# A banded product in four 64x64 tiles of TensorE, in two stacked banded layers (one core of a Trainium2)

## The chip, the cores and the metric

The kernel runs on one NeuronCore of one Trainium2 chip. The metric is the device time of one execution in microseconds; the time before the change is 4874.15 us, the median of 3 runs (4872.71 to 4876.42). In the profile PE is TensorE's matmuls, PEld its weight loads, DVE VectorE, ACT ScalarE, POOL GpSimd and SP the SyncE queue, which here issues nearly all DMAs.

## The reference

The input x is 512 x 512 positions of 64 channels. Two layers of one form follow each other, each with weights of its own:

```python
def layer(x):                                  # x: (1, 512, 512, 64)
    xn   = ln(group_norm(x, 32 groups))        # per position, over 64 channels
    left  = (xn @ Wl + bl) * mask * sigmoid(xn @ Wlg + blg)     # 64 -> 128
    right = (xn @ Wr + br) * mask * sigmoid(xn @ Wrg + brg)
    gate  = sigmoid(xn @ Wog + bog)
    out = 0
    for dd in range(-4, 5):                    # band of nine rows
        out[i, j] += left[i + dd, i] * right[i + dd, j]          # per channel
    out = ln(out) * gate
    return x + out @ Wo + bo                   # 128 -> 64
```

The statistics of the group norm run over the whole image, so the second layer can begin its work only when the first is through. The band couples only the nine rows around row i, and of left only the positions (i + dd, i) near the diagonal are needed. For one channel, the sum over dd is a product of a banded 64 x 64 matrix (from left) with rows of right.

## The kernel before, in words

**Tiling.** The 512 rows are cut into nine blocks of 64 rows that overlap by eight. A tile holds on its 128 partitions the 64 rows of a block twice: partitions 0 to 63 for a column j, 64 to 127 for column j + 256. These are the two halves, `e` = 0 and 1 in the code. A *unit* is 8 columns of each half, a *chunk* 16 units (128 columns of each half), so a layer has 18 chunks or 288 units. All arithmetic is fp32.

**One step.** `layer` (line 718) writes out one unit step after the other; nearly every instruction is recorded through one helper at line 373, which keeps all of them in program order, so the profile shows L373 everywhere and groups are told apart by tiles. In step t of a layer:

- `affine`, `inner_stats`, `inner_norm` (427 to 440): group norm and layer norm of z on POOL, statistics on DVE. `solve` (577), every fourth step, turns the statistics into the scales: five small instructions on DVE (var, nm, rs), then a chain of ten to twelve on POOL (rsqrt, rs, nm).
- `transposed`, `kept` (442, 461): PE transposes z into PSUM, ACT copies it to SBUF as zT (adding 1.0, by which the biases enter the products), SP stores zT to `later` in DRAM.
- `right` (488), `right_gate`, `right_end`: twice per step, PE multiplies zT by the right weights and their gate weights (4 matmuls of 64 rows x 128 columns of weights, 256 moving columns), ACT takes the sigmoid (sg), DVE multiplies into RO.
- `mix` (544): the band product, for 8 channels of a chunk. Per channel and half one matmul of 64 x 64 weights (A, from left) and 128 moving columns of RO; result in two PSUM banks, then copied back over RO, one half by ACT and one by DVE. 16 mixes per chunk, laid out over ten of its 16 steps as 2,1,2,2,1,2,1,2,2,1 (line 743).
- `out_stats`, `norm` (571, 610): statistics of the product on DVE, normalisation on ACT (eight instructions of 128 x 128 per step, tile `on`).
- `recall`, `gates`, `gated` (619 to 645): zT read back 30 steps later as zg, multiplied by the gate weights, sigmoid on ACT.
- `turned`, `times_gate`, `end` (647 to 695): transposes of the normalised product, times gate on DVE (ZH), times Wo on PE. `fetch`, `biased`, `ended`: x is fetched into XR, biased on POOL, added on DVE, stored by SP. In layer 0 `sums` (706) adds up on PE the statistics for the next group norm.

**Left.** `left` (502) runs in steps 3, 5, 7, 9 and 11 of each layer for the 36 near-diagonal positions, and writes its result to DRAM (`left_of`), in the layout in which `take_left` (532) fetches 16 channels (a *slab*) into a tile A of 64 positions x 16 channels per partition, the same for both halves.

**What sets the order.** Each engine works its own list in program order. The lists follow the order of the calls in the loop of `layer`. `count` (line 761) says how many units' affines fall in each of a chunk's 16 steps: 1,1,2,1,2,1,1,2,1,1,1,0,1,1,0,0. PSUM has eight banks: two pairs (`two_banks`, line 131) that right, transposed and mix share, and single ones (`one_bank`, line 128) for gates, turned and end: three in layer 0 (an eighth bank holds the sums), four in layer 1. A request waits until the oldest tile of its ring is free.

Of the kernel before, what the change touches and what calls it, by code (L numbers as in the profile page):

```python
# [8 lines left out]
F32 = mybir.dt.float32  # L9
# [10 lines left out]
S = 64  # L20
# [59 lines left out]
def tile_two_banded_layers(  # L80
# [28 lines left out]
    slab = S * (S + 2 * WIN) * HA  # L109
    size = H // HA * slab  # L110
# [350 lines left out]
    def kept(u: Unit):  # L461
        u.t = ztp.tile([P, JU // 2, P], F32, tag="zT", name="zT")
        to = u.t.rearrange("c k (n p) -> c n k p", n=2)
        for n, pt in enumerate(u.pt):
            en.scalar.activation(
                to[:, n : n + pt.shape[1]], pt.rearrange("c n (k p) -> c n k p", p=S),
                AF.Identity, bias=1.0,
            )
        if u.near is None:
            en.sync.dma_start(later[u.at], u.t)  # L470
# [5 lines left out]
    def projected(u: Unit, q: int, w: bass.AP):  # L476

        pr = two_banks().rearrange("p (e k h) -> p e k h", e=2, k=JQ // 2)
        for k in range(JQ // 2):
            for e in range(2):  # L480
                part = slice(e * D, (e + 1) * D)
                en.tensor.matmul(
                    pr[:, e, k, :], lhsT=u.t[part, q // 2 + k, :], rhs=w[part],
                    start=True, stop=True,
                )
        return pr

    def right(u: Unit, q: int, w: dict):
        u.pr[q] = projected(u, q, w["right"]).rearrange("p e k h -> p (e k) h")
# [12 lines left out]
    def left(u: Unit, q: int, w: dict):  # L502

        n0 = u.near + q
        pr = projected(u, q, w["left"])
        sg = wk.tile([P, JQ, H], F32, tag="sg", name="sg", bufs=2)
        sl = sg.rearrange("p j h -> p (j h)").rearrange("p (s j x) -> p s j x", j=JQ, x=HA)
        sv = sl.rearrange("p s (k e) x -> p e k s x", e=2)
        for e in range(2):
            en.scalar.activation(  # L510
                sv[:, e], pr[:, e, :, H:].rearrange("p k (s x) -> p k s x", x=HA), AF.Sigmoid
            )
        near = w["near"][:, n0 : n0 + JQ].unsqueeze(1).unsqueeze(3)
        en.gpsimd.tensor_tensor(sl, sl, near.broadcast_to([P, H // HA, JQ, HA]), ALU.mult)
        for e in range(2):
            en.vector.tensor_tensor(
                sv[:, e], pr[:, e, :, :H].rearrange("p k (s x) -> p k s x", x=HA), sv[:, e],
                ALU.mult,
            )
        for o, r, k, m in runs(n0, n0 + JQ):  # L520
            for n, b in enumerate(blocks):
                q0 = b.s // JQ
                at = n * size + (r * (S + 2 * WIN + 1) + k) * HA
                en.sync.dma_start(
                    strided(
                        left_of, at, (JQ * (S + 2 * WIN + 1) * HA, S // JQ), (slab, H // HA),
                        (1, m * HA),
                    ),
                    sl[q0 : q0 + S // JQ, :, o : o + m, :].rearrange("q s j x -> q s (j x)"),
                )  # L530

    def take_left(n: int, h: int) -> bass.AP:


        A = lp.tile([P, S, HA], F32, tag="A", name="A")
        at = n * size + h * slab + WIN * HA
        for e in range(2):
            en.sync.dma_start(
                A[e * S : (e + 1) * S].rearrange("p i h -> p (i h)"),
                strided(left_of, at, ((S + 2 * WIN) * HA, S), (1, S * HA)),  # L540
            )
        return A

    def mix(c: int, A: bass.AP, h0: int) -> list:


        j0 = c % 2 * (JC - JW)
        R = RO[:, :, j0 : j0 + JC, :]
        pb = two_banks()
        ph = pb.rearrange("i (h j) -> i h j", j=JC)  # L550
        for turn in range(2):
            for h in range(HB // 2):
                for e in range(2):
                    part = slice(e * S, (e + 1) * S)
                    hh = (turn ^ e) * (HB // 2) + h
                    en.tensor.matmul(
                        ph[part, hh, :], lhsT=A[part, :, h0 % HA + hh],
                        rhs=R[part, (h0 + hh) // 2, :, hh % 2],
                        start=True, stop=True,
                    )  # L560
        q = HB // 4
        v = [pb.rearrange("i (h t j) -> i h j t", t=2, j=JC)[:, n * q : (n + 1) * q] for n in range(2)]
        return [(R[:, h0 // 2 + n * q : h0 // 2 + (n + 1) * q], v[n]) for n in range(2)]
# [154 lines left out]
    def layer(src: bass.AP, dst: bass.AP, w: dict, stats: bool, then=None):  # L718
# [60 lines left out]
        for t in range(min(loads), last_t + 3):  # L779
# [37 lines left out]
            if t in units:  # L817
                right(units[t], 0, w)
            if t in outs:
                gates(outs[t], w)  # L820
            for v in looking[0:2]:
                out_stats(*v)
            if t in units:
                right_gate(units[t], 0)
            for u in inputs(t + 2):
                inner_norm(u)
            if t in units:
                right_end(units[t], 0)
            if t in outs:
                gated(outs[t])  # L830
# [4 lines left out]
            if t in units:  # L835
                right(units[t], JQ, w)
            for v in looking[2:5]:
                out_stats(*v)
            if t in outs:
                turned(outs[t], w)  # L840
            for u in inputs(t + 1):
                transposed(u)
            for u in then_affine:
                affine(u, en.gpsimd)
            then_affine = []
            if stats and t - 2 in outs:
                sums(outs[t - 2], t - 2 == first_t, t - 2 == last_t)
            for v in looking[5:]:
                out_stats(*v)
            if t - 1 in outs:  # L850
                end(outs[t - 1], w)
            if t in units:
                right_gate(units[t], JQ)
            if t + 1 in outs:
                norm(outs[t + 1], 0, 4)
            for u in inputs(t + 1):
                kept(u)
            if t in units:
                right_end(units[t], JQ)
            for v in todo:  # L860
                inner_stats(*v)
            if len(mixing) > 0:
                c, h0 = mixing[0]
                mixed.append(mix(c, A[c, h0 // HA], h0))
# [6 lines left out]
            if t in outs:  # L871
                times_gate(outs[t], w)
            if len(mixing) > 1:
                c, h0 = mixing[1]
                mixed.append(mix(c, A[c, h0 // HA], h0))
            if t + 1 in outs:
                norm(outs[t + 1], 4, 8)
            if len(mixing) > 0:
                en.scalar.copy(*mixed[0][0])
            if len(mixing) > 1:  # L880
                en.scalar.copy(*mixed[1][0])
            if t - 1 in outs:
                ended(dst, outs[t - 1])
            if len(mixing) > 0:
                en.vector.tensor_copy(*mixed[0][1])
            if t in outs:
                biased(outs[t], w, stats)
# [78 lines left out]

    XR = [keep.tile([P, JU // 2, 2 * D + 2], F32, name=f"XR{i}") for i in range(4)]
# [56 lines left out]
```

## Time and profile before

| | us |
|---|---|
| median of 3 runs | 4874.15 |
| the profiled execution, its time | 4876.42 |
| its span in the profile | 4874.6 |
| statistics of the input (POOL idle, DVE at work) | 0 to 290 |
| start of layer 0, with `left` | 290 to 440 |
| first mixes | 440 to 550 |
| steady steps of layer 0 | 550 to 2400 |
| last steps of layer 0 | 2400 to 2600 |
| start of layer 1, first mixes | 2600 to 2870 |
| steady steps, then last steps of layer 1 | 2870 to 4710, to 4875 |

How to read it. The page gives for each engine its busy time and share of the span, then for the costliest groups the number of instructions, the busy time in us, the mean length of one in ns, and the engine's idle time just before them with its releaser. A table of stretches gives the busy time of every engine between two moments. An instruction's busy time can overlap its successor's on PE and ACT, so the sum over groups may exceed an engine's busy time. The view of waits names who waited for whom. In the timeline equal instructions that follow each other are merged (x32).

### The profile page before, as it was taken

To read this page: it belongs to the slowest core of one execution; us is meant where nothing else is said; L and a number is where in the kernel's file an instruction comes from. 1 tells how busy PE (TensorE), PEld (TensorE's weight loads), DVE (VectorE), ACT (ScalarE), POOL (GpSimd) and SP (SyncE) were. 2 spreads that over 40 slices of the span, in tenths; PEclk is the share of its full clock that TensorE was granted. 3 is DMA by queue.
4 is the path that set the end of the run, shared out by engine and by line. 5 is a ranking of instruction groups with operands and counts; after the bars stand their busy time and mean duration, and the time that the engine had idled before them with its cause. 6 is when DMAs were issued, how large, how long until landed. Compare 5 with 4: busy or idle time off the path is not lost.

```text
span 4874.6 us, 173394 instructions
## 1 busy us (share of the span) xinstructions
PE 4107.5 (84%) x67090; PEld 3507.8 (72%) x67090; DVE 3830.6 (79%) x9635; ACT 3642.8 (75%) x8156; POOL 3804.8 (78%) x4739
## 2 busy tenths in 40 slices
PE   1026899999999999999984589999999999999998
PEld 0014788888888888888863467777777777777786
DVE  6835788888888888888765578888888888888887
ACT  0013688888888888888872368888888888888888
POOL 0035899989999999999634589998999999998963
PEclk9987999999999999999996899999999999999999
DMA  7844577777777777777653457777777777777766
GB/s 302 338 161 118 164 212 212 211 207 211 207 215 211 209 208 210 212 212 213 188 161 86 118 166 215 209 211 205 209 208 213 211 208 209 207 211 212 218 191 172
DMA packets 905343, 982.31 MB, mean 202 GB/s; under 512 B 114210, under 2 KB 641608, under 8 KB 900168
## 3 DMA queue, kind: packets, MB, share of 16 engines
q1 hardware_dynamic: 899840, 969.73, 68.0%
q8 instruction: 530, 8.68, 0.8%
q14 instruction: 293, 2.40, 0.2%
q10 hardware_dynamic: 4680, 1.50, 0.1%
HBM read 658.42 MB, written 312.46 MB: 199 GB/s over the span
## 4 chain that ended last, share of the span: by engine, by line
PE 56%; DVE 15%; ACT 12%; POOL 6%; DMA 4%; issue 3%; SPq 3%; ACTq 0%; POOLq 0%; DVEq 0%
PE banks L373 36%; PE bank L373 18%; ACT on L373 6%; DVE gn_st L373 3%; POOL rsqrt L373 3%; DVE RO L373 3%; SPq L373 3%; PE acc L373 3%; DVE sto L373 3%; ACT gate L373 2%; ACT zT L373 2%; DVE sti L373 2%; DVE ZH L373 2%; ACT sg L373 1%; DVE var L373 1%
## 5 line engine op out<-in xcount | busy, mean ns | idle before, releaser
L373 ACT ACTIVATE on<-RO,nm,rs 128x128 f32<-128x128 f32 x4608 | 1924.3, 492 | 68.3 <-POOL nm L373 53.7
L373 PE MATMUL banks<-pack,zT 64*128 64x256 f32 x9360 | 1335.1, 407 | 358.1 <-ACT zT L373 281.3
L373 PEld LDWEIGHTS banks<-pack,zT 64*128 64x128 f32 x9360 | 893.5, 195 | 731.7 <-ACT zT L373 327.8
L373 PE MATMUL banks<-RO,A 64*64 64x128 f32 x18432 | 1154.5, 277 | 19.9 <-ACT zT L373 12.7
L373 PEld LDWEIGHTS banks<-RO,A 64*64 64x64 f32 x18432 | 1082.5, 183 | 46.9 <-ACT zT L373 15.2
L373 DVE TENSOR_TENSOR RO<-banks,sg 128x512 f32<-128x512 f32 x1152 | 788.2, 684 | 396.3 <-ACT sg L373 376.4
L373 ACT ACTIVATE sg<-banks 128x512 f32<-128x512 f32 (+1 forms) x1188 | 697.1, 588 | 421.9 <-PE banks L373 292.5
L373 DVE BATCH_NORM_STATS2 sto<-RO 128x6 f32<-128x256 f32 x2304 | 845.2, 413 | 1.2
L373 DVE SCALAR_TENSOR_TENSOR ZH<-bank,pack,gate 128x448 f32<-128x448 f32 (+1 forms) x1152 | 736.4, 681 | 44.6 <-ACT gate L373 27.8
L373 DVE COPY RO<-banks 128x512 f32<-128x512 f32 x576 | 397.8, 691 | 430.0 <-ACT RO L373 427.7
L373 POOL TENSOR_TENSOR z<-z,gb 128x512 f32<-128x512 f32 x536 | 686.0, 1280 | 42.0
L373 POOL TENSOR_TENSOR z<-z,ga 128x512 f32<-128x512 f32 x536 | 685.2, 1278 | 5.6 <-DMA z<-mid_x 2.4
L373 PE MATMUL bank<-pack,ZH 128*64 128x64 f32 x18432 | 651.4, 224 | 4.7 <-ACT gate L373 4.3
L373 POOL TENSOR_TENSOR z<-z,rs 128x512 f32<-128x512 f32 x586 | 613.1, 1046 | 46.0
L373 ACT ACTIVATE gate<-bank 128x448 f32<-128x448 f32 (+1 forms) x1152 | 570.3, 547 | 88.1 <-PE bank L373 81.9
L373 POOL TENSOR_TENSOR z<-z,sti 128x512 f32<-128x512 f32 x586 | 620.8, 1059 | 0.0
L373 PEld LDWEIGHTS bank<-pack,ZH 128*64 128x64 f32 x18432 | 587.2, 138 | 26.3 <-ACT gate L373 7.9
L373 PE MATMUL bank<-zg,pack 64*128 64x448 f32 (+1 forms) x2304 | 568.7, 561 | 2.6 <-DMA zg<-later 2.3
L373 ACT COPY RO<-banks 128x512 f32<-128x512 f32 x576 | 335.1, 582 | 284.3 <-PE banks L373 280.0
L373 DVE BATCH_NORM_STATS2 sti<-z 128x6 f32<-128x128 f32 x2344 | 504.2, 282 | 12.9 <-POOL z L373 12.7
L373 PEld LDWEIGHTS bank<-ident,on 64*128 64x128 f32 x9216 | 404.9, 139 | 125.7 <-ACT gate L373 36.7
L373 POOL TENSOR_TENSOR XR<-XR,pack 120x512 f32<-120x512 f32 (+1 forms) x352 | 417.8, 1189 | 86.5 <-DMA XR<-in_x_dram 32.0
(145 smaller groups left out, 3587.2 us busy)
## 6 DMA issues: line engine op xcount, KB each, us to landing
later<-zT SPq DMA_DIRECT2D x576, 256.0 KB
A<-left_of SPq DMA_DIRECT2D x576, 256.0 KB
zg<-later SPq DMA_DIRECT2D x576, 256.0 KB
z<-in_x_dram SPq DMA_DIRECT2D x576, 128.0 KB
z<-mid_x SPq DMA_DIRECT2D x576, 128.0 KB
gn_x<-in_x_dram SPq DMA_DIRECT2D x16, 4096.0 KB
XR<-in_x_dram SPq DMA_DIRECT2D x448, 112.0 KB
mid_x<-XR SPq DMA_DIRECT2D x448, 112.0 KB
```

The costliest lines, as they stand in the source:

```text
L373: return lambda *a, **k: tc.keep_in_program_order(f(*a, **k))
```

## The change

It does the same arithmetic with four edits.

1. **The band product in four tiles.** Of the 128 channels, half (`s` = 1) are kept with swapped halves: the row half e of RO holds for them the columns of half 1 - e. In `mix` the matmul for these channels reads rows of half e and writes partitions of half 1 - e (`to` = `e ^ s`), so that the four 64x64 tiles (row half, column half) are each addressed in turn, and the result comes out with its halves in place. `one_bank` is asked twice per mix, one bank for s = 0 and one for s = 1; `two_banks` is no longer used for it.
2. **`crossed`, in place of `projected`, for right.** The swapped channels are made at the projection: zT is kept with its first half once more behind the second (`P + S` columns, a third ACT copy in `kept`), and right's matmul for s = 1 takes the weights' window shifted by 64. There are eight matmuls of 128 moving columns per call instead of four of 256.
3. **Left as channel pairs.** `left` writes its product into L9, a view of the last 36 columns of RO, which are not in use yet, and sends it out when all nine positions of a row offset r are there. `take_left` fetches A as 8 pairs x 64 positions x 2, in four transfers per slab instead of two.
4. **Another order of the calls in a step.** `out_stats`, `inner_stats` and `solve` stand ahead of `gated` and `right_end`; `gates` and both `right` calls follow each other; the mixes come late, the second behind the second half of `norm`, with `sums` between `end` and the second mix.

From the programs' lists: SP issues 72 transfers `left_of<-RO` of 16 x 64 runs of 18 numbers in place of 216 `left_of<-sg` of 16 x 8 runs of 16 to 64 numbers, and 1152 `A<-left_of` of 64 x 4 runs of 128 numbers in place of 576 of 64 runs of 1024.

```diff
     def kept(u: Unit):
-        u.t = ztp.tile([P, JU // 2, P], F32, tag="zT", name="zT")
-        to = u.t.rearrange("c k (n p) -> c n k p", n=2)
+        u.t = ztp.tile([P, JU // 2, P + S], F32, tag="zT", name="zT")
+        to = u.t.rearrange("c k (n p) -> c n k p", n=3)
...
         if u.near is None:
-            en.sync.dma_start(later[u.at], u.t)
+            en.scalar.activation(
+                to[:, 2], u.pt[0][:, 0].rearrange("c (k p) -> c k p", p=S), AF.Identity, bias=1.0
+            )
+            en.sync.dma_start(later[u.at], u.t[:, :, :P])
...
+    def crossed(u: Unit, q: int, w: bass.AP):
+        pr = two_banks().rearrange("p (e k h) -> p e k h", e=2, k=JQ // 2)
+        for k in range(JQ // 2):
+            for s in range(2):
+                for e in range(2):
+                    part = slice(e * D, (e + 1) * D)
+                    en.tensor.matmul(
+                        pr[:, e, k, :].rearrange("p (g s x) -> p g s x", g=2, s=2)[:, :, s],
+                        lhsT=u.t[part, q // 2 + k, s * S : s * S + P],
+                        rhs=w[part].rearrange("c (g s x) -> c g s x", g=2, s=2)[:, :, s],
+                        start=True, stop=True,
+                    )
+        return pr
...
     def left(u: Unit, q: int, w: dict):
...
         for e in range(2):
             en.vector.tensor_tensor(
-                sv[:, e], pr[:, e, :, :H].rearrange("p k (s x) -> p k s x", x=HA), sv[:, e],
-                ALU.mult,
+                L9[:, :, n0 + e : n0 + JQ : 2, :],
+                pr[:, e, :, :H].rearrange("p k (h t) -> p h k t", t=2),
+                sv[:, e].rearrange("p k (h t) -> p h k t", t=2), ALU.mult,
             )
-        for o, r, k, m in runs(n0, n0 + JQ):
-            for n, b in enumerate(blocks):
...
+        for r in range(JQ):
+            if n0 < (r + 1) * NEAR <= n0 + JQ:
+                for n, b in enumerate(blocks):
...
     def take_left(n: int, h: int) -> bass.AP:
-        A = lp.tile([P, S, HA], F32, tag="A", name="A")
+        A = lp.tile([P, HA // 2, S, 2], F32, tag="A", name="A")
...
     def mix(c: int, A: bass.AP, h0: int) -> list:
...
-        pb = two_banks()
-        ph = pb.rearrange("i (h j) -> i h j", j=JC)
-        for turn in range(2):
-            for h in range(HB // 2):
-                for e in range(2):
-                    part = slice(e * S, (e + 1) * S)
-                    hh = (turn ^ e) * (HB // 2) + h
-                    en.tensor.matmul(
-                        ph[part, hh, :], lhsT=A[part, :, h0 % HA + hh],
-                        rhs=R[part, (h0 + hh) // 2, :, hh % 2],
-                        start=True, stop=True,
-                    )
+        ph = [one_bank().rearrange("i (h t j) -> i h t j", h=q, t=2) for s in range(2)]
+        for h in range(q):
+            for t in range(2):
+                for s in range(2):
+                    for e in range(2):
+                        part, to = (slice(n * S, (n + 1) * S) for n in (e, e ^ s))
+                        en.tensor.matmul(
+                            ph[s][to, h, t, :], lhsT=L[part, s, h, :, t], rhs=R[part, s, h, :, t],
+                            start=True, stop=True,
+                        )
...
+    L9 = RO[:, :, 2 * JC - JW - NEAR * JQ :, :]
```

The order of the calls in a step, steady part, each engine's own list (before, then after; "t" left out where it is the step's own unit):

```
PE    before: right0 gates right1 turned transposed(t+1) sums(t-2) end(t-1) mix mix
PE    after:  right0 gates right1 turned transposed(t+1) end(t-1) mix sums(t-2) mix
DVE   before: looks right_end0 looks right_end1 inner_stats solve times_gate ended copy copy
DVE   after:  looks inner_stats solve right_end0 times_gate right_end1 ended copy copy
ACT   before: sg0 gated sg1 norm kept norm copy copy
ACT   after:  sg0 gated sg1 norm kept kept' copy norm copy
POOL  before: inner_norm affine affine(t+1) rsqrt biased
POOL  after:  inner_norm affine rsqrt biased affine(t+1)
```

## The prediction

> **What bounds the kernel now.** I read the page's busy times first, then stretches from the middle of each layer, then one engine at a time: who waits, and for how long.
>
> ```profile
> PE 4107.5 (84%) x67090; PEld 3507.8 (72%) x67090; DVE 3830.6 (79%) x9635; ACT 3642.8 (75%) x8156; POOL 3804.8 (78%) x4739
> ```
>
> Five rows between 72% and 84% bound nothing by themselves. The table of stretches (PE, PEld, DVE, ACT, POOL busy us, then clock and DMA) does better:
>
> ```profile
> 1000.00:2000.00 1000.00, 963.97 (x17089) 853.27 (x17084) 834.46 (x2101) 866.50 (x1929) 912.95 (x1107) 1.00 0.74 210
> 3200.00:4200.00 1000.00, 918.65 (x14834) 785.64 (x14832) 843.03 (x2093) 856.01 (x1922) 911.96 (x1105) 0.98 0.74 209
> ```
>
> The first row is layer 0, the second layer 1, which does without the sums on PE: 45 us less PE busy, yet the same number of steps. The sg tile, two per step, counts 275 and 275 on ACT: 137.5 steps, 7.27 us each, 116.3 us for a chunk of 16. So PE, though busiest, does not set the pace alone. POOL's busy time leaves out a gap of some 80 ns behind most of its instructions; its waits are this (us, times, longest):
>
> ```profile
> POOL rsqrt L373 <- DVE rs L373: 32.8, 35, 1.9
> POOL z L373 <- DMA z<-in_x_dram: 0.9, 2, 0.5
> ```
>
> POOL waits 33.7 us in 1000, once in each solve. The rest, 966 us, is its own: 7.03 us a step, 112.4 a chunk. And most of those waits are not DVE being late:
>
> ```profile
> 1523.43 1.28 POOL L373 TENSOR_TENSOR z<-z,gb 128x512 f32<-128x512 f32 x1
> ...
> 1524.35 0.40 DVE L373 TENSOR_SCALAR var<-sti 128x32 f32<-128x32 f32 x1
> ...
> 1525.11 0.20 DVE L373 TENSOR_SCALAR rs<-var 128x64 int32<-128x64 int32 x1
> ...
> 1525.38 0.29 POOL L373 TENSOR_TENSOR rsqrt<-rs 128x64 f32<-128x64 f32 x1 [0.67 <-DVE rs L373]
> ```
>
> DVE's first solve instruction takes 0.40 us here and 0.16 us where POOL is idle; it ends as POOL's gb ends, and POOL then sits out the rest of the solve. By start times this 0.67 to 0.79 us repeats in three solves of four; only the solve after the mixes waits longer, 1.6 to 1.9 us. 4 waits x about 0.95 us = 3.9, and 112.4 + 3.9 = 116.3: **POOL sets the pace**, with PE level with it in the mixing steps.
>
> **The change, part by part.**
>
> *The band product.* Of one pair of mixes the timeline says, and of the product with Wo just ahead of it the groups:
>
> ```profile
> 1506.72 3.94 PE L373 MATMUL banks<-RO,A 64*64 64x128 f32 x64
> ```
> ```profile
> L373 PE MATMUL bank<-pack,ZH 128*64 128x64 f32 x18432 | 651.4, 224 | 4.7 <-ACT gate L373 4.3
> L373 ACT ACTIVATE zT<-bank 128x256 f32<-128x256 f32 x16 | 5.2, 384 | 1.8 <-PE bank L373 1.8
> ```
>
> A mix is 32 records in 1.97 us. In the trace's start times they begin two at a time, 6 ns apart, a pair every 109 ns: two tiles at work. Entering or leaving the 64x64 shape costs some 0.2 us (152 ns to the first record, then 214 instead of 109). After, 16 groups of four would be 8 x 109 = 0.87 us, plus 0.2. No row shows four tiles at once: at best 1.07 us a mix, at worst the 1.97 of now. Two row halves (right) run in pairs, and so do two column halves (Wo, pairs 52 ns apart for 64 columns); so I take 1.07, 0.9 us of PE a step. The Trainium skill ("TensorEngine Tiling (Array Packing)", Gotcha 1: PSUM Pressure) speaks against this: different row tiles cannot access one PSUM bank at the same time. After the change both row halves write one bank, on different partitions, where now each has its own; by that rule the 0.9 us would be nothing. No row here tests it.
>
> *The crossed projection* doubles right's matmuls at half the columns. Right is now 8 records, pairs 209 ns apart for 256 columns; at 128 columns the mix shows 109. So 8 pairs x 109 instead of 4 x 209 is 0.04 us per half, 0.07 per step. Weight loads of 128 columns run every 62 ns per pair in the transposes, under 109: hidden. Two more shape changes a step in layer 0 (sums now lie between end and mix): 0 to 0.4 us.
>
> *The third copy of zT* is 0.38 us (row above) on ACT, in each step. ACT is busy 866.5/137.5 = 6.30 us per step; it becomes 6.65. In steps without a mix ACT and PE already run a closed loop (the chain of waits goes zT, right, gate, sg, norm, zT), 5.6 us long; I count 0.35 us there, so 6.0.
>
> *The order in a step.* DVE now solves before its right_end; today it solves late. POOL meanwhile keeps inner_norm, affine, rsqrt, biased, with the next step's affine after rsqrt. So rsqrt should find rs ready, and the 3.9 us a chunk of waits goes. What is late next: a unit's affine costs POOL 2.56 us (1.279 and 1.280, its two rows) and the rest of a step 7.03 - 2.56 = 4.47. By the table of affines the ten mixing steps have 13 of a chunk's 16 units, so POOL's work there is 10 x 4.47 + 13 x 2.56 = 78 us; ACT's is 10 x (6.65 - 0.53) + 16 x 0.53 = 70, DVE's 10 x (6.07 - 0.69) + 16 x 0.69 = 65, PE's 10 x 5.1 + 16 x 1.07 = 68 (0.53 and 0.69 are the copies of a mix, 6.07 and 5.1 the busy times per step, PE's without its mix). POOL is the slowest there; over the six others ACT's 6 x 6.0 = 36 stands against POOL's 34.5. Whether a chunk gets to 112.4 depends on how far the others can run ahead of POOL. inner_stats now stands early in DVE's queue, with right_end, times_gate, ended and the copies behind it, and it needs POOL's affine of the step before; I reckon 1 to 3.6 us of lead, so 112.4 to 115. I take 113.9, **-2.4 us x 30 chunks = -72 us** (bounds: -117 if POOL never waits, +50 if lead is nil and ACT adds its 0.35 x 6 in full).
>
> *The left factor's way out.* SP at the start of layer 0:
>
> ```profile
> 334.51 9.52 SPq L373 DMA_DIRECT2D left_of<-sg  x18
> ...
> 357.20 12.68 SPq L373 DMA_DIRECT2D left_of<-sg  x27
> ...
> 380.53 12.85 SPq L373 DMA_DIRECT2D left_of<-sg  x27
> ...
> 405.14 12.65 SPq L373 DMA_DIRECT2D left_of<-sg  x27
> ...
> 428.41 5.20 SPq L373 DMA_DIRECT2D left_of<-sg  x9
> ```
>
> That is 108 issues, 52.9 us of SP, and z's loads stand behind them; ACT also waits 50.4 us in 290:440 until sg has landed, all engines being under half busy. After: 36 issues from L9, and sg is free once DVE has multiplied. Each has 1024 runs of 72 bytes instead of 128 of 64 to 256. A's issue (64 runs) takes 0.55 us, XR's (224 runs) 0.50: flat, so 36 x 0.47 = 17 us, -36. If price went with runs, 128 runs per 0.47 us, 36 would cost 135 us, +82. The flat rows are nearer; some of the saving is not on the path: **-28 us a layer, -56.** The skill ("DMA: Bandwidth & Descriptors", Specifications) says that under 512 B a transfer is read, modified and written. In this trace's packet records 64-byte packets took 9 ns and 256-byte ones 22 ns, no penalty, so I charge 25 us of queue time beside other work.
>
> *A in pieces.* Per slab 1024 runs of 512 bytes instead of 128 of 4096. The trace's packets: 8 x 29 = 232 ns against 253, so nothing on the DMA queue (74% busy). SP issues four transfers, not two: 0.55 us per step more on about 4.6; hidden, since slabs are asked for more than two steps early. Uncovered it would be that 0.55 us x 288 steps.
>
> *Ends.* While chunk 1 fills, POOL is busy 103 of 110 us: -2 a layer. The last mixes, with no units left, run in 5.6 to 8.6 us steps where ACT needs about 5.4: -8 a layer. Together -20.
>
> **Sum.** 4876.4 (the profiled execution; its span is 4874.6, the median of the runs 4874.15, 0.05% below) - 72 - 56 - 20 = **4728 us**.
>
> **Rivals.** (a) *POOL gapless*: chunk 112.4, so -117 - 72 (the start in full) - 20: **4667**. For: its waits are the smallest of any engine. Against: ACT's loop in six steps. (b) *POOL locked*: no lead, steady steps as now, only start and ends: **4800**. (c) *Slower: ACT becomes the bound.* ACT waits now 1.0 us a step (sg 41.2, copies 63.7, gate 15.9 and on 8.6 us in 1000: 0.94). If the new order keeps these waits, its step is 6.65 + 0.97 = 7.62, +0.35 x 16 x 30 = +168, less 76: **4968**. It decides once ACT's waits exceed 0.62 us per step. For: layer 0 has three single banks for seven to nine requests a step, and gates now needs the last ACT copy's bank. Against: two norm halves lie behind the mixes, as cover. (d) *Slower: four tiles run as two.* Mix stays 1.97; shape changes and crossing add 0.25 us a step in layer 0, 0.05 in layer 1: +60 +12, start -56: **4892**. It decides if a mix takes over 1.6 us. The change does then not do what it says.
>
> **Chances.** The forecast 0.42 (own range 4695 to 4770), (a) 0.15, (b) 0.16, (c) 0.13, (d) 0.09, and 0.05 that gains and costs cancel within 0.2%, which is about what a measurement of this kernel can tell from no change. Faster 0.73, same 0.05, slower 0.22. The range takes in (a), (b), (d) and the left factor's upper price on part of the start: 4660 to 4895; it leaves (c) out.
>
> **What would show it.** A mix's records in groups of four and x32 in about 1.1 us; POOL's waits for DVE rs well under 33 us in 1000; SP's left issues x9, below 5 us each time; ACT busy near 93% in the steady stretches. I am wrong if ACT's waits grow instead, if the left issues take over 1.4 us each, or if POOL's instructions themselves get longer.

## The result, and the profile after

The changed kernel takes 4813.48 us (median of 4 runs, 4808.51 to 4821.80) beside 4875.28 for the kernel before (4 runs): ratio 0.9873, 95% interval 0.9856 to 0.9891, so 62 us or 1.27% faster. The forecast was 4728, 148 us faster. The profiled execution took 4808.51 us, its span is 4806.5, against 4874.6: -68.1.

The page's first part (busy us, share of the span, instructions), and the two steady stretches (PE, PEld, DVE, ACT, POOL busy, then clock, DMA share, GB/s):

```profile
PE 3796.6 (79%) x76306; PEld 3293.0 (69%) x76306; DVE 3929.9 (82%) x9635; ACT 3708.4 (77%) x8732; POOL 3817.1 (79%) x4739
```
```profile
1000.00:2000.00 1000.00, 915.40 (x19402) 808.53 (x19400) 853.16 (x2101) 890.67 (x2073) 917.87 (x1103) 0.98 0.76 211
3200.00:4200.00 1000.00, 841.95 (x17340) 739.23 (x17340) 888.88 (x2133) 875.49 (x2094) 927.56 (x1119) 0.96 0.77 213
```

PE, first before, is now level with POOL in all and far below it in layer 1: 919 became 842 in 1000 us. POOL rose from 913 to 918 and from 912 to 928. ACT rose by 24 and 19, to 89.1 and 87.5% of these stretches; the prediction's sign for it was 93%. The waits of POOL for DVE's solve (us, times, longest), in layer 0 and then layer 1, were 32.8 and 33.5:

```profile
POOL rsqrt L373 <- DVE rs L373: 29.3, 34, 1.9
...
POOL rsqrt L373 <- DVE rs L373: 18.5, 24, 1.7
```

The group of the band product before and after (count, busy us, mean ns of one, idle before): 706.0 / 576 = 1.23 us a mix, where it was 1154.5 / 576 = 2.00.

```profile
L373 PE MATMUL banks<-RO,A 64*64 64x128 f32 x18432 | 1154.5, 277 | 19.9 <-ACT zT L373 12.7 <-DVE RO L373 7.2
...
L373 PE MATMUL bank<-RO,A 64*64 64x128 f32 x18432 | 706.0, 292 | 3.9 <-ACT RO L373 2.4
```

And SP's queue at the start of layer 0, the left factor's way out: 36 issues, 50.4 us in all, where 108 issues took 52.9. The prediction's sign was below 5 us for each nine.

```profile
344.71 10.83 SPq L373 DMA_DIRECT2D left_of<-RO  x9
...
367.76 15.12 SPq L373 DMA_DIRECT2D left_of<-RO  x9
...
397.06 14.56 SPq L373 DMA_DIRECT2D left_of<-RO  x9
...
426.63 9.85 SPq L373 DMA_DIRECT2D left_of<-RO  x9
```

Where the 68 us came from, read from the times at which SP issues each step's store of zT (us; "left16" and "short" are experiments below):

| part of the span | before | after | forecast of the difference | difference | left16 | short |
|---|---|---|---|---|---|---|
| layer 0, first 32 steps | 250.4 | 241.2 | -30 | -9.2 | 205.0 | 206.9 |
| layer 0, next 240 steps | 1743.7 | 1733.0 | -36 | -10.7 | 1734.5 | 1717.9 |
| last 16 steps, change of layers | 322.6 | 312.9 | -8 | -9.7 | 313.4 | 310.5 |
| layer 1, first 32 steps | 248.7 | 245.2 | -30 | -3.5 | 201.1 | 203.9 |
| layer 1, next 240 steps | 1742.6 | 1715.1 | -36 | -27.5 | 1714.2 | 1703.4 |
| last 16 steps and tail | 260.6 | 251.3 | -8 | -9.3 | 251.5 | 249.8 |

The ends came as forecast. The starts gave 13 us instead of 60, the steady steps 38 instead of 72.

### The profile page after: what moved, and what is told of

Its sections match the earlier page's. It is cut to its first block, busy times and chain, and to the rows that moved or that the text cites. A ratio compares the mean times of both kernels' runs of the same rounds, so it can differ in the third digit from the quotient of the medians.

```text
span 4806.5 us, 193543 instructions
## 1 busy us (share of the span) xinstructions
PE 3796.6 (79%) x76306; PEld 3293.0 (69%) x76306; DVE 3929.9 (82%) x9635; ACT 3708.4 (77%) x8732; POOL 3817.1 (79%) x4739
## 5 line engine op out<-in xcount | busy, mean ns | idle before, releaser
L373 PEld LDWEIGHTS banks<-pack,zT 64*128 64x128 f32 x18576 | 1251.3, 195 | 549.5 <-ACT zT L373 288.9
L373 PE MATMUL banks<-pack,zT 64*128 64x128 f32 x18576 | 1365.6, 289 | 272.8 <-ACT zT L373 222.6
L373 DVE TENSOR_TENSOR RO<-banks,sg 128x512 f32<-128x512 f32 (+1 forms) x1188 | 795.3, 673 | 228.3 <-POOL sg L373 116.2
L373 DVE BATCH_NORM_STATS2 sto<-RO 128x6 f32<-128x256 f32 x2304 | 800.8, 411 | 3.7
L373 PE MATMUL bank<-RO,A 64*64 64x128 f32 x18432 | 706.0, 292 | 3.9 <-ACT RO L373 2.4
L373 DVE COPY RO<-bank 128x512 f32<-128x512 f32 x576 | 398.4, 692 | 310.6 <-PE bank L373 307.3
L373 PEld LDWEIGHTS bank<-RO,A 64*64 64x64 f32 x18432 | 582.0, 142 | 43.0 <-ACT RO L373 4.1
L373 ACT ACTIVATE zT<-banks 128x512 f32<-128x512 f32 (+1 forms) x1084 | 463.5, 481 | 139.6 <-PE banks L373 128.9
L373 ACT COPY RO<-bank 128x512 f32<-128x512 f32 x576 | 333.2, 579 | 282.3 <-PE bank L373 282.1
L373 PE MATMUL banks<-ident,z 64*128 64x64 f32 x4336 | 254.1, 233 | 359.2 <-DVE RO L373 336.9
```

The costliest lines, as they stand in the source:

```text
L373: return lambda *a, **k: tc.keep_in_program_order(f(*a, **k))
```

## The experiments

The kernel before took 4875 to 4879 us beside each of them. The steady chunk of each run (16 steps, mean of chunks 4 to 17, layer 0 / layer 1) stands beside a sum: POOL's own 112.4 us a chunk, divided by one minus the share of all POOL's waits in 1000:2000 and 3200:4200.

| run | time, us | ratio to before (95%) | POOL's waits in 1000 us | sum | chunk measured |
|---|---|---|---|---|---|
| before | 4875 | | 33.7 / 34.8 | 116.3 / 116.5 | 116.3 / 116.3 |
| after | 4813.5 | 0.9873 (0.9856 to 0.9891) | 29.5 / 18.5 | 115.8 / 114.5 | 115.6 / 114.4 |
| left16 | 4735.7 | 0.9705 (0.9691 to 0.9718) | 30.6 / 17.0 | 115.9 / 114.3 | 115.6 / 114.3 |
| two_tiles | 4913.2 | 1.0065 (1.0052 to 1.0078) | 60.4 / 20.0 | 119.6 / 114.7 | 119.5 / 114.9 |
| old_order | 5108.8 | 1.0470 (1.0455 to 1.0484) | 108.2 / 61.2 | 126.0 / 119.7 | 126.4 / 119.7 |
| new_order_only | 5501.9 | 1.1270 (1.1255 to 1.1286) | 179.5 / 164.7 | 137.0 / 134.6 | 136.6 / 134.9 |
| l16_pair | 5000.3 | 1.0258 (1.0244 to 1.0272) | 88.0 / 92.9 | 123.2 / 123.9 | 123.4 / 123.3 |
| l16_two_copies | 4724.5 | 0.9688 (0.9675 to 0.9701) | 28.3 / 15.7 | 115.7 / 114.2 | 115.5 / 114.2 |
| l16_solve | 4734.1 | 0.9709 (0.9696 to 0.9722) | 33.7 / 19.9 | 116.3 / 114.7 | 116.0 / 114.4 |
| l16_biased | 4766.3 | 0.9774 (0.9760 to 0.9787) | 33.0 / 31.4 | 116.2 / 116.0 | 116.5 / 115.9 |
| l16_then | 4807.8 | 0.9851 (0.9839 to 0.9864) | 48.9 / 37.1 | 118.2 / 116.7 | 118.2 / 116.7 |
| l16_then_lend | 4873.9 | 0.9989 (0.9979 to 0.9999) | 80.1 / 71.1 | 122.2 / 121.0 | 120.2 / 119.4 |
| l16_short | 4702.9 | 0.9634 (0.9621 to 0.9647) | 17.9 / 10.2 | 114.5 / 113.5 | 114.5 / 113.5 |

The sum holds within 0.6 us for 24 chunks of 113 to 137 us; l16_then_lend, which takes work from POOL, is the exception (with the 109.8 us expected there its sum is 119.4 / 118.2). It is bookkeeping: it says that POOL's own work stayed what it was and that POOL stood still only in waits that the profile names. It says where to look, POOL's waits, and not what causes them.

**1. left16: the left factor in longer runs.**

```diff
-    L9 = RO[:, :, 2 * JC - JW - NEAR * JQ :, :]
+    L9 = RO[:, : H // HA * JQ, 2 * JC - JW - NEAR * HA // 2 :, :].rearrange(
+        "p (l r) j t -> p l r (j t)", r=JQ
+    )
...
-                            left_of, at, (JQ * (H // 2 * span + 2), S // JQ), (span, H // 2),
-                            (1, 2 * NEAR),
+                            left_of, at, (JQ * (S + 2 * WIN + 1) * HA, S // JQ), (slab, H // HA),
+                            (1, NEAR * HA),
...
-        A = lp.tile([P, HA // 2, S, 2], F32, tag="A", name="A")
+        A = lp.tile([P, S, HA], F32, tag="A", name="A")
```

> The changed kernel, but with left kept and sent out as slabs of 16 channels: 36 issues of 128 runs of 576 bytes a layer instead of 36 of 1024 runs of 72, and A fetched in two transfers of 64 runs of 4096 bytes instead of four of 256 runs of 512. Theory (an issue is priced by its runs, and SP's time there stands on the path): the 36 issues take about 36 x 0.47 = 17 us a layer instead of 50.4, the first 16 steps of a layer become 28 to 33 us shorter than now (149.1 and 150.8 us), time 4813 - 56 to - 66 = 4747 to 4757 us. Rival 1 (an issue has a flat price, and what made the nine issues long is something else, a wait in the queue): the issues stay at 1.2 to 1.7 us each and the time at 4813. Rival 2 (SP is not on the path there): the issues get short, the first 16 steps stay within 8 us of now, time 4800 to 4815.

4735.7 us, 78 below after. SP's queue at the start of layer 0:

```profile
345.85 4.88 SPq L373 DMA_DIRECT2D left_of<-RO  x9
...
360.30 4.28 SPq L373 DMA_DIRECT2D left_of<-RO  x9
...
376.12 4.16 SPq L373 DMA_DIRECT2D left_of<-RO  x9
...
391.58 4.17 SPq L373 DMA_DIRECT2D left_of<-RO  x9
```

36 issues take 17.5 us (19.5 in layer 1), 0.49 each, where the same 36 took 50.4. The next nine issues now follow after 14 to 16 us instead of 23 to 30, and the first 32 steps of a layer are 36 and 44 us shorter, with the steady chunks unchanged. So SP's time was on the path, and rival 2 falls. The theory's size was too small: the first 16 steps became 44 and 49 us shorter, not 28 to 33, and the time fell below its range. The other edit of this run, A in half as many issues, can have little part in it: in after, A's issues begin only at 446.9 us, 139 us into the first 16 steps.

What made the issues long is less a price by runs, as the theory has it, than the wait in the queue of rival 1. Of the second nine issues of after, then of left16, the shortest, the median and the longest (ns):

```profile
L373 SPq DMA_DIRECT2D left_of<-RO x9: 308/1186/3820, 367.8 to 380.6; - x9
```
```profile
L373 SPq DMA_DIRECT2D left_of<-RO x9: 308/437/545, 360.3 to 364.1; - x9
```

In each nine of after the first issue took 0.31 to 0.34 us and the second 0.55 to 0.56, with 1024 runs each; in left16, with 128 runs, the first took the same 0.31 to 0.34. Only from the third on do the long lists take 0.56 to 3.82 us. By itself an issue of 1024 runs is therefore about as short as one of 128; the later ones stand behind the runs handed over before them. The stretch 290:440 of before and of after shows these runs being moved (the last three numbers: clock, DMA share, GB/s):

```profile
290.00:440.00 150.00, 69.19 (x462) 52.83 (x464) 74.75 (x189) 35.70 (x87) 67.21 (x97) 0.73 0.29 74
```
```profile
290.00:440.00 150.00, 64.34 (x680) 56.74 (x680) 83.64 (x190) 38.92 (x99) 78.03 (x102) 0.74 0.72 68
```

The packets' time rose from 29% to 72% of that of the 16 DMA engines, for fewer bytes a second. In the packet records the 36,864 packets of 72 bytes took 32 ns each on average (median 12), 74 us of 16 engines; the 64-byte packets of before took 9 ns. In left16 the 4608 packets of 576 bytes took 47 ns, 13 us of 16 engines. So it was rival 1's cause, and its forecast fell because fewer runs ended the wait. What holds the queue is not separated: while the second nine of after were moved (367.7 to 389.3) the share was 1.30, as packets overlap, which is a full queue; with the first nine (344.7 to 359.0) it was 0.75. Why a packet of 72 bytes took so much longer than one of 64 no run here asks.

**2. two_tiles: the product without four tiles at once.**

```diff
-        for h in range(q):
-            for t in range(2):
-                for s in range(2):
+        for s in range(2):
+            for h in range(q):
+                for t in range(2):
```

> The changed kernel with one loop of the band product turned outward, so that the 16 matmuls of s = 0 come first and those of s = 1 after them: only two of the four tiles can be at work at once; all else as it is. Theory (four tiles do run at once, but POOL sets the steady pace, so most of the gain on PE is hidden): a mix of 32 records goes from 1.23 back to 1.8 to 2.0 us, PE 0.6 to 0.75 us a step busier, and the time rises only by 0 to 45 us, to 4813 to 4860. Rival 1 (PE on the path, the mix is where the gain comes from): 16 mixes a chunk x 0.7 = 11 us x 36 chunks = +400, 5200 us; already over 4950 would speak for it. Rival 2 (1.23 us has another reason than four tiles): the mix stays at 1.2 us, time 4813.

4913.2 us, 100 above after, more than the theory allowed and far from the 400 of its first rival; the second rival falls with the mix. The group's row:

```profile
L373 PE MATMUL bank<-RO,A 64*64 64x128 f32 x18432 | 907.5, 283 | 1.2 <-ACT RO L373 0.6 <-DVE ZH L373 0.6
```

907.5 / 576 = 1.58 us a mix, not 1.8 to 2.0: the trace's start times show the end of the 16 matmuls of s = 0 beside the beginning of s = 1, so the loop order only takes part of the overlap away. 0.35 us x 16 = 5.6 us more of PE a chunk made the chunk 3.9 us longer in layer 0 and 0.5 in layer 1, where PE has no sums to do. In layer 0 the shorter mix was thus not hidden. In the 240 steps of the table that is 58 + 8 of the 94 us of span. Some 23 more lie in the first 32 steps, where SP's 36 left issues took 57.0 us in layer 0 instead of 50.4, though nothing about them was changed: their 72-byte packets took 41 ns on average here, and 32 in after.

**3. old_order and new_order_only: one half of the change without the other.** The first takes the changed functions and puts the calls in the order of before, the second the functions of before in the changed order (the two lists under "The change"). Of the first:

```diff
-            if t in outs:
-                times_gate(outs[t], w)
...
             if len(mixing) > 0:
                 c, h0 = mixing[0]
                 mixed.append(mix(c, A[c, h0 // HA], h0))
...
+            if t in outs:
+                times_gate(outs[t], w)
```

> The changed kernel's product, projection, third copy and left factor, in the order of calls of the kernel before. Theory (the order is what makes the steady steps shorter, by an earlier solve): POOL's waits for DVE rs in its solve are back at about 33 us in 1000 in both layers, the steady chunk at 116.3 us or above (third copy), time 4860 to 4900. Rival (the product and the rest make the gain, the order nothing): time 4805 to 4825.

> The kernel before with the changed order of calls alone: band product in two tiles, right in four matmuls, left out in 108 issues. Theory (the order gives the steady gain, but the late mixes of 2.0 us, which hold two banks of the pair ring, take part of it back): steady chunks 114 to 117 us, time 4815 to 4880, and with the start not dearer by the left issues. Rival 1 (the order does it all): 4800 to 4815. Rival 2 (the order does nothing without the shorter mix): 4875 or above.

5108.8 and 5501.9 us: each half alone is much slower than the kernel before (+230 and +624), together they gain 62. No theory of mine had that; 5501.9 lies in the open range of the last rival, which spoke of no effect and not of a loss. The waits in 1000:2000, of old_order and then of new_order_only:

```profile
PEld bank L373 <- DVE ZH L373: 120.4, 160, 2.1
...
POOL rsqrt L373 <- DVE rs L373: 83.0, 31, 5.9
PE bank L373 <- DVE ZH L373: 78.0, 79, 2.0
```
```profile
DVE RO L373 <- ACT RO L373: 256.7, 118, 3.4
ACT RO L373 <- PE banks L373: 222.6, 119, 4.1
POOL rsqrt L373 <- DVE rs L373: 171.1, 29, 9.5
```

These causes are read from the waits; of old_order no run tests them. In old_order the mixes ask the ring of three or four single banks and get one only when times_gate (ZH), which the old order calls behind the first mix, has emptied it: of the 439 us for which PE stands idle ahead of mixes, 362 end with ZH. In new_order_only the late mixes wait for the pair ring, and their two copies run one after the other: DVE's copy begins when ACT's has ended. The semaphores in the trace say why: where both halves of a mix lie in one tile of two banks, DVE's copy waits for ACT's semaphore; where each half is a tile of its own, it waits for PE's alone. This is a dependence that the program sets, not the chip. It was there before too (DVE RO for ACT RO, 107.3 us in 1000), at a lower price in the old order.

**4. l16_pair: is it the banks, or the 2.0 us mix?** The kernel of run 1 with the result back in a pair:

```diff
-        ph = [one_bank().rearrange("i (h t j) -> i h t j", h=q, t=2) for s in range(2)]
+        pb = two_banks().rearrange("i (s h t j) -> i s h t j", s=2, h=q, t=2)
+        ph = [pb[:, s] for s in range(2)]
```

> The kernel of run left16 (4735.7 us), with the result of a mix in the two halves of one pair of banks (the ring that right and the transposes use), as in the kernel before, in place of two single banks; four tiles and the new order stay. Theory (new_order_only was slow because of the banks: the copies of a mix read one tile, so DVE's copy waits for ACT's to end, and the pair stays taken meanwhile): DVE's waits for ACT RO come back at over 100 us in 1000 and POOL's for DVE rs at over 80, time 4950 to 5400. Rival (new_order_only was slow because of the 2.0 us mix): DVE's copies start with ACT's or cost nothing, time 4735 to 4800.

5000.3 us, 265 above left16. The same three waits come back, in 1000:2000:

```profile
DVE RO L373 <- ACT RO L373: 172.7, 128, 1.9
ACT RO L373 <- PE banks L373: 113.3, 82, 2.8
POOL rsqrt L373 <- DVE rs L373: 87.8, 33, 4.2
```

In left16 DVE's copies wait 91.4 us in 1000, and for PE, not for ACT. So in the new order, with the mix short in both, putting the result back into a pair costs 265 us, and the theory holds. The run changes two things at once, the tile that two engines read and the ring that it comes from, and does not separate them. The prediction has no term for this part of the change.

**5. l16_two_copies: the third copy of zT.**

```diff
-            en.scalar.activation(
-                to[:, 2], u.pt[0][:, 0].rearrange("c (k p) -> c k p", p=S), AF.Identity, bias=1.0
-            )
...
-                        lhsT=u.t[part, q // 2 + k, s * S : s * S + P],
+                        lhsT=u.t[part, q // 2 + k, :P],
```

> The kernel of run left16 (4735.7 us) without the third ACT copy of zT; right's matmuls for s = 1 take the unshifted window instead, so that the swapped channels hold the columns of the wrong half; all other work is the same. Theory (POOL sets the steady pace and ACT, busy 88 to 89%, lies beside it): the 0.37 us a step come off ACT, the time falls by 0 to 40 us, to 4695 to 4736. Rival 1 (ACT is the bound, or the loop zT, right, sg, norm): 0.37 x 16 x 30 = 178 us, of which over 90 would show, 4560 to 4645. Rival 2 (no effect at all): 4730 to 4740.

What this kernel leaves out is the copy that puts the swapped halves in place, so its result is not the layer's; the other work is that of left16. It took 4724.5 us, 11 below left16 (12.6 of span): 6 in the two starts (205.0 to 200.0 and 201.1 to 200.0), 4.4 in the 480 steady steps. 0.37 us of ACT a step is nearly free: ACT does not set the pace.

**6. Why POOL still waits for the solve.** The trace of after around two solves, DVE and POOL (start, us, then what; in brackets the idle time before and its releaser):

```profile
1507.27 1.27 POOL L373 TENSOR_TENSOR z<-z,ga 128x512 f32<-128x512 f32 x1
1507.62 0.97 DVE L373 TENSOR_SCALAR var<-sti 128x32 f32<-128x32 f32 x1
1508.51 0.18 DVE L373 SCALAR_TENSOR_TENSOR var<-sto,pack 128x32 f32<-128x32 f32 x1
1508.62 1.26 POOL L373 TENSOR_TENSOR z<-z,gb 128x512 f32<-128x512 f32 x1
1508.72 1.20 DVE L373 TENSOR_SCALAR var<-var 128x32 f32<-128x32 f32 x1
...
1510.23 0.29 POOL L373 TENSOR_TENSOR rsqrt<-rs 128x64 f32<-128x64 f32 x1 [0.35 <-DVE rs L373]
...
1537.59 0.69 DVE L373 COPY RO<-bank 128x512 f32<-128x512 f32 x1 [1.04 <-PE bank L373]
...
1541.08 0.17 DVE L373 TENSOR_SCALAR var<-sti 128x32 f32<-128x32 f32 x1
...
1541.88 0.29 POOL L373 TENSOR_TENSOR rsqrt<-rs 128x64 f32<-128x64 f32 x1 [1.01 <-DVE rs L373]
```

At 1507.62 DVE's solve starts early, as the new order wants, and is held: the instruction of 0.17 us takes 0.97 and ends some 40 ns after POOL's ga, the third slips in, the next, 0.18 us long elsewhere, takes 1.20 and ends with POOL's gb. POOL then waits for what is left. Coming earlier does not by itself put DVE ahead of POOL; it did in some solves of layer 1, where POOL waited 24 times in 1000 us instead of 34. At 1541.08 it is simply late: the copy of the second mix waited 1.04 us for PE. By start times, on average, the four solves of a layer 0 chunk made POOL wait 0.78, 0.69, 1.76 and 0.68 us before, and 0.69, 0.35, 1.16 and 1.10 after.

Four edits of left16 tried this wait. l16_solve writes three of the held instructions with a second operand:

```diff
-            en.vector.tensor_scalar(vo, vo, LN_EPS, None, ALU.add)
+            en.vector.tensor_tensor(vo, vo, eps.broadcast_to([P, no]), ALU.add)
```

> The kernel of run left16 (4735.7 us), with three of solve's four TENSOR_SCALAR instructions on DVE (var from sti, var plus eps, nm) written as instructions with a second operand from SBUF (a column of eps or of -1), same arithmetic and order. Theory (what holds them till the end of POOL's instruction is their form with a single SBUF operand): these three take 0.16 to 0.2 us each time, also beside POOL, POOL's waits for DVE rs fall from 30 and 17 us in 1000 to under 15 and 9, time 4680 to 4715. Rival (any DVE instruction that reads only SBUF is held beside POOL, or these are held for another reason): their durations still reach 0.9 to 1.2 us and the time stays at 4725 to 4745.

4734.1 us, no change, and no shorter lengths (540 ns where TENSOR_SCALAR var<-var had 540; nm rose from 173 to 272):

```profile
L377 DVE TENSOR_TENSOR var<-var,eps 128x32 f32<-128x32 f32 x144 | 77.7, 540 | 5.0
```

My theory of the form is wrong; the rival holds, but not for "any instruction that reads only SBUF": BATCH_NORM_STATS2, SBUF to SBUF, took 267 to 301 ns whether POOL was at work or not, and those with a PSUM operand were not held either. The Trainium skill has it so ("SBUF — State Buffer", Who interferes with whom): DVE contends with GpSimd when it reads two SBUF inputs, and tensor_scalar can in its two-port mode; the whole instruction is then waited out. These runs agree: DVE's held instructions ended 35 to 54 ns behind POOL's in after and left16.

l16_biased and l16_then put POOL work between the affine that holds the solve and rsqrt: `biased`, or the next step's affine. The call that moves, of the one and of the other:

```diff
+            if t in outs:
+                biased(outs[t], w, stats)
             if t % 4 == 0:
                 st, us = sti.pop((t + 4) // 4, (None, []))
...
-            if t in outs:
-                biased(outs[t], w, stats)
```
```diff
+            for u in then_affine:
+                affine(u, en.gpsimd)
+            then_affine = []
             if t % 4 == 0:
                 st, us = sti.pop((t + 4) // 4, (None, []))
```

> The kernel of run left16 (4735.7 us), with the call of biased moved ahead of solve, which moves one POOL instruction of 1.18 us from behind the rsqrt chain to ahead of it, and nothing else. Theory (POOL sets the steady pace, and its remaining waits for DVE rs, 30 us in 1000 in layer 0 and 17 in layer 1, come from DVE's solve being held by POOL's own last instruction before rsqrt): one more instruction in between lets the solve through, the waits fall below 10 in 1000, the steady chunk from 115.6 and 114.3 to 112.5 to 114, time 4670 to 4710. Rival 1 (DVE is held by whatever POOL does, so the wait moves along): waits and time as in left16, 4725 to 4745. Rival 2 (a later rsqrt makes PE, which waits 46 us in 1000 for POOL's rsqrt, wait longer): 4745 to 4800.

> The kernel of run left16 (4735.7 us), with the next step's affine (two POOL instructions of 1.28 us, every fourth step) called ahead of solve instead of behind it; only POOL's list changes, and inner_norm of the next step stays where it is. Theory (a chunk takes POOL's own 112.4 us over 1 minus the share of its waits, which gave every steady chunk measured so far within 0.6 us): the solve's waits of 30 and 17 us in 1000 fall below 10, biased waits for nothing because it stays behind rsqrt, chunks of 112.6 to 113.6 us in both layers, time 4735 - 15 x 2.5 - 15 x 1.2 = 4680, 4665 to 4700. Rival 1 (rsqrt 2.6 us later makes norm later, so turned, end and the copies are late and the waits come back at the next solve, as run l16_biased gave them back at XR): POOL's waits together stay at 25 to 35 in 1000, 4735 to 4770. Rival 2 (DVE is held once more by the two added instructions): waits for rs as now, 4725 to 4745.

4766.3 and 4807.8 us: both slower, by 31 and 72, the second above every range given for it. POOL's waits in 3200:4200, of l16_biased:

```profile
POOL XR L373 <- DMA XR<-mid_x: 19.6, 13, 2.6
POOL rsqrt L373 <- DVE rs L373: 6.4, 13, 0.7
```

The solve's wait did fall, from 17.0 to 6.4 and, in l16_then, 7.7, and a wait for XR took its place (19.6 and 18.1). For l16_biased that is its own move, biased asking earlier for the fetched x. Its time lies in the range of its rival 2, and that rival's sign came too: PE's weight loads waited 53.5 and 60.4 us in 1000 for POOL's rsqrt, where they had waited 46.2 and 43.7. Which of the two costs the 31 us is open. For l16_then I can only argue it: with rsqrt 2.6 us later what follows is later, the ring of four XR turns later, and biased stands still for it. l16_then_lend, which also gave one affine of a chunk to DVE:

```diff
-            for u in affines.pop(t, []):
-                affine(u, en.vector if u.at < NU + 4 else en.gpsimd)
+            for n, u in enumerate(affines.pop(t, [])):
+                lend = n == 1 and t > NU and t % NU == 7
+                affine(u, en.vector if u.at < NU + 4 or lend else en.gpsimd)
```

> As run l16_then, and one unit's affine of a chunk (the second one in the step 7 of 16) worked by DVE instead of POOL. Theory (POOL's own work sets the pace): 2.56 + 0.1 us less for POOL per chunk, 109.8 instead of 112.4; DVE gains two instructions of 0.81 and 1.04 us, or up to 1.3 each where POOL holds them, at 85 to 89% busy; 2.0 to 2.6 us a chunk under l16_then, 60 to 80 us. Rival (DVE's queue in that step is on the path of ZH, XR and the copies, and gives it back): l16_then's time or up to 40 us above it.

4873.9 us (ratio to before 0.9989, 0.9979 to 0.9999), 66 above l16_then; POOL's waits for DVE rs grew from 18.0 and 7.7 to 52.2 and 44.8 in 1000. The way is the rival's, the cost more than its 40 us: what POOL no longer did it waited for at DVE.

l16_short moves nothing. It shortens the solve ahead of rs by two instructions, this one and nm's, which is called behind rs:

```diff
-                vo.rearrange("p (k t) -> p k t", t=2), sto[:, :, 2::3], 1.0 / H,
-                w["m2"][:, js].rearrange("p (k t) -> p k t", t=2), ALU.mult, ALU.mult,
-            )
-            en.vector.tensor_scalar(vo, vo, LN_EPS, None, ALU.add)
+                vo.rearrange("p (k t) -> p k t", t=2), sto[:, :, 2::3], H * LN_EPS,
+                w["m2"][:, js].rearrange("p (k t) -> p k t", t=2), ALU.add, ALU.mult,
+            )
```

> The kernel of run left16 (4735.7 us) with a shorter solve on DVE ahead of rs: the instruction that adds eps is folded into the one before it (whose factor 1/H goes into the mask row at the start), and nm, which POOL needs only at the end of its chain, comes behind rs. No engine's list is otherwise changed and POOL's order stays. In left16 rs ends 0.67 us behind the POOL instruction that held the solve, in four more instructions; two of them go, some 0.35 us, and the second hold of 1.1 us in one solve of four with them. Theory (a steady chunk is POOL's own 112.4 us plus its waits, and this wait has its cause in the solve): waits for DVE rs from 30 and 17 us in 1000 to 14 to 20 and 4 to 9, chunks of 113.8 to 114.8 and 113 to 113.7 us, time 4695 to 4722. Rival (POOL is level with the other engines, and what it gains here it waits for elsewhere, as in the runs l16_biased and l16_then): waits for XR or z appear, chunks and time stay within 0.3 us of 115.6 and 114.3, 4728 to 4745 or above.

```profile
POOL rsqrt L375 <- DVE rs L375: 9.2, 14, 1.9
POOL rsqrt L375 <- DVE nm L375: 8.7, 12, 1.8
```

4702.9 us, as the theory said: 33 below left16, chunks of 114.5 and 113.5, waits for the solve of 17.9 us in layer 0 (the two rows above, in 1000:2000) and 10.2 in layer 1, where 4 to 9 was expected. About half of the rest is now put down to nm, the next instruction behind rs on DVE. This is the best version found, 3.7% under the kernel before. The wait for the solve is a real cost; it could be made shorter, but not moved out of the way.

## Why the prediction was wrong, point by point

- **The left factor's way out: the step that failed most.** "A's issue (64 runs) takes 0.55 us, XR's (224 runs) 0.50: flat, so 36 x 0.47 = 17 us", and beside it only "25 us of queue time beside other work". Instead 36 issues cost 50.4 us. The flat price as such held (0.31 us for a first issue of 1024 runs). The term that was mis-sized, as far as the records show, is the moving of the runs: it was charged from packets of 64 bytes (9 ns) and 256 (22 ns), but the 72-byte packets took 32, 74 us of 16 engines and not 25, and not beside other work, since SP stood in its issues meanwhile. Of the 60 us for the two starts 13 came; left16 brought 93. The upper bound, 135 us, was as far off on the other side. SP on the path: right.
- **The order in a step: -72 became -38.** "So rsqrt should find rs ready" failed. The prediction quoted the row that speaks against it (0.40 us "as POOL's gb ends") and took it for a late start, not for a hold that goes wherever the solve goes. "POOL's waits for DVE rs well under 33 us in 1000" came half true: 18.5 in layer 1, 29.3 in layer 0, where the late second mix also makes DVE late. (Its bound of +50 does not follow from its own terms: 0.35 x 6 x 30 is 63.)
- **POOL sets the pace: fits, not fully shown.** The table's sum holds in all versions with POOL's own work unchanged, 0.37 us of ACT a step was nearly free, and a shorter solve gave 33 us. But in layer 0 a longer mix on PE lengthened the chunk by way of POOL's waits, and the one run that took work from POOL, l16_then_lend, got slower.
- **The band product: near in size** (1.07 forecast, 1.23 measured); the fours start mostly 115 ns apart, and so did the pairs of before (114 in the mix that the prediction quotes), where its sum took 109. The skill's rule against it ("TensorEngine Tiling (Array Packing)", Gotcha 1: PSUM Pressure) did not hold here: two row halves write one bank at once. Rival (d), four tiles as two, is out; the overlap that two_tiles takes away, 0.35 us of the 0.77 gained, costs 66 us of steady steps, so the shorter mix is far less hidden than I had it in the new order.
- **Banks apart: not priced at all.** The prediction summed product and order as independent terms, and neither works without the other: 5108.8 and 5501.9 us. With both, but the banks in a pair, left16 becomes 5000.3.
- **The crossed projection** was put at 0.07 us a step; the group of right went from 1335.1 to 1365.6 us, 0.05 a step. **The third copy**: nearly free, so rival (c), ACT the bound, is out. **A in pieces**: four issues of 256 runs, 2.7 us a slab instead of 1.1, hidden in the steady steps as said (left16's chunks are the same). **Ends**: -8 a layer forecast, -9.7 and -9.3 measured; the ramp's own part cannot be told from the start's.
- **Rival (b), 4800, is nearest** in its number, by luck: it keeps the steady steps and gains the start, where the chip gained steady steps and ends and little of the start. (a) fell with the waits.

Open: why layer 0 kept more of its waits than layer 1. The sums on PE, which delay the second mix and so DVE, fit it; no run took them away.

## What to carry to other kernels

An issue's price taken from a queue that keeps up does not carry to a burst that fills it: count the runs handed over together, and what each packet of that size takes. Where an engine's wait follows another engine's instruction that ends with its own, ask whether the two hold each other before moving anything; shortening that work helps, placing it earlier may not. And parts of a change that share a ring of buffers are not terms of a sum: price the pair, or say that you cannot.

## What the runs showed of the hardware that I had not expected

- An issue on SP's queue took a median of 0.43 us with 128 runs (left_of in before and left16), 0.59 with 64 and 0.62 with 256 (A in before and in after), 0.31 with 1024 as the first of nine and 0.55 as the second; from the third on the issues of 1024 runs took 0.56 to 3.82 us. The same 36 took 50.4 us in after, 56.4 in old_order, 57.0 in two_tiles.
- Packets of 72 bytes took 32 ns on average in after and 41 in two_tiles (median 12 in both), where packets of 64 bytes took 9 in before.
- Small DVE instructions with SBUF operands (0.16 to 0.2 us) stretched to 1.2 us beside POOL, ending 35 to 54 ns after POOL's instruction, while BATCH_NORM_STATS2 was never held.
- Four 64x64 tiles at work at once, with two row halves writing different partitions of one bank: in the mix of after at 1501.91 us the first matmuls of the eight fours start 0, 170, 286, 402, 515, 627, 740 and 855 ns from the first; in before it was pairs that started some 114 ns apart.
